# Graph attention in f32: keys on the partitions, heads packed into the array's row and column groups, the mask as a factor

## Chip, cores, metric

One core of a Trainium2 chip. The metric is device time in microseconds of one execution; medians of several executions are given. All runs told of here were in the fast state. Ratios are the mean time of one kernel's fast runs over that of the other's of the same rounds, so they are not quite the ratio of the medians quoted.

## The reference, cut to what matters

32 graphs of 512 nodes with 256 channels, f32 throughout. Two layers of masked attention with 8 heads of 32 channels; in layer 0 the mask is the symmetrised graph with its diagonal, in layer 1 the directed graph. Layer 0 has an MLP of 1,024 channels as well, and norms stand between.

```python
# layer 0 (inside: attention, norm, MLP, norm), then layer 1
x = _layernorm(x + _L0_gnn_ref(x, adj, ...))
x = _layernorm(x + _L1_gnn_ref(x, adj, ...))
# attention in both, with q, k, v as [graph, head, node, 32]
scores = einsum(q, k) / sqrt(32)
scores = where(allowed, scores, -inf)
out = einsum(softmax(scores), v)
```

## The kernel before

Two graphs are in work at a time, as two streams of pieces that a scheduler puts in order on each engine. Queries are on the partitions. For 128 queries and two heads:

```python
for j in range(2):                                   # L229: the mask, added in PSUM
    nc.tensor.matmul(s[:, j, :], ident_b, mask[:, i, :], start=True, stop=False)
for j, h in enumerate(heads):                        # L232: scores, 32 rows of the array
    at = slice((h % HPC) * HD, (h % HPC + 1) * HD)
    nc.tensor.matmul(s[:, j, :], qT[at, ...], kT[at, ...], start=False, stop=True)
nc.vector.tensor_reduce(top[...], s, AX.X, ALU.max, negate=True)            # L235
for j, h in enumerate(heads):                        # L238: exp, and the row sums
    nc.scalar.activation(p[:, j, :], s[:, j, :], AF.Exp, bias=top[:, h:h+1], accum_out=total[:, h:h+1])
# ... later, for each head
for k in range(NQ):                                  # L249: p transposed
    nc.tensor.transpose(ps[:, k*P:(k+1)*P], p[:, j, k*P:(k+1)*P], ident)
evict(pT, ps)                                        # L130 / L132, ScalarE and VectorE in turn
for k in range(NQ):                                  # L253: 32 columns for each 128-column weight
    nc.tensor.matmul(acc[:, h*HD:(h+1)*HD], pT[:, k*P:(k+1)*P], v[:, k, h*HD:(h+1)*HD], ...)
```

## Time and profile before

| | before |
|---|---|
| median | 10,242 us (10,190 to 10,266) |
| span in the profile | 10,250 us |
| TensorE busy | 10,080 us, 98% |
| VectorE / ScalarE / GpSimd busy | 3,223 / 2,375 / 1,234 us |
| mean granted TensorE clock | 0.711 |

A busy TensorE row is not an array at its peak: the same matmul takes twice as long at half the granted clock (one head's scores 1.051 us and 2.001 us, medians of this trace). So the clock is read beside the busy time. The prediction below quotes the lines.

### The profile page before, as it was taken

Reading aid. Unit: us, or ns where it says so; the run is one execution under the profiler, and the core shown is the slowest. Engines: PE = TensorE matmul, PEld = TensorE weight load, DVE = VectorE, ACT = ScalarE, POOL = GpSimd, SP = SyncE. Lnnn points to the kernel's source line nnn. Section 1 sums busy time; section 2 is a strip of 40 time slices with the busy share of each in tenths; the row PEclk is TensorE's granted clock in tenths of the full one; section 3 lists DMA queues with packets and bytes.
Section 4 is the critical chain, followed back from the end, with each engine's and each line's share of the span. In section 5 each row is a group of like instructions: output and inputs, shape, how many; then the busy total and the mean of one; then the engine's idle time right before and its main releaser. Section 6 shows DMA issues by size and latency. Waiting matters only on the chain.

```text
span 10250.1 us, 92945 instructions
## 1 busy us (share of the span) xinstructions
PE 10079.9 (98%) x38912; PEld 6353.5 (62%) x38912; DVE 3223.0 (31%) x5233; ACT 2374.8 (23%) x5681; POOL 1233.6 (12%) x1575
## 2 busy tenths in 40 slices
PE   9999999999999999999999999999999999999999
PEld 5666666656666666666666666666666666666665
DVE  2333333333332333323333233332333323333232
ACT  1222222222222222222222222222222222222221
POOL 2001111011110111101111011110011100111000
PEclk7667777677776777767777677776677767777666
DMA  1000000000000000000000000000000000000000
GB/s 44 7 3 9 9 9 7 3 9 9 9 7 3 9 9 9 7 3 9 9 9 9 1 9 9 9 9 5 5 9 9 9 5 5 9 9 5 1 3 5
DMA packets 57477, 78.44 MB, mean 8 GB/s; under 512 B 3936, under 2 KB 40160, under 8 KB 57056
## 3 DMA queue, kind: packets, MB, share of 16 engines
q1 hardware_dynamic: 57056, 72.50, 2.2%
q8 instruction: 304, 4.98, 0.2%
q14 instruction: 117, 0.96, 0.0%
HBM read 55.71 MB, written 16.78 MB: 7 GB/s over the span
## 4 chain that ended last, share of the span: by engine, by line
PE 92%; DVE 4%; POOL 3%; issue 1%; ACT 1%; DMA 0%; POOLq 0%; ACTq 0%; SPq 0%; DVEq 0%
PE psS L232 26%; PE psA L253 25%; PE psP L249 14%; PE psS L229 7%; PE psH L320 5%; PE psQK L197 4%; PE psO L279 4%; PE psF L330 2%; PE psV L206 2%; PE psC L274 1%; DVE top L235 1%; POOL rs L142 1%; PE psT L166 1%; POOL edge L176 1%; DVE st L139 1%; POOL rs L141 1%
## 5 line engine op out<-in xcount | busy, mean ns | idle before, releaser
L253 PEld LDWEIGHTS psA<-v,pT 128*128 128x128 f32 x16384 | 2723.0, 252 | 1250.5 <-issue 794.7
L232 PE MATMUL psS<-kT,qT 32*128 32x512 f32 x4096 | 2906.4, 911 | 0.0
L253 PE MATMUL psA<-v,pT 128*128 128x32 f32 x16384 | 2814.8, 329 | 69.4 <-DVE pT L132 60.9
L235 DVE TENSOR_REDUCE top<-psS 128x2 f32<-128x1024 f32 x1024 | 1253.0, 1224 | 2741.9 <-PE psS L232 2741.9
L249 PEld LDWEIGHTS psP<-ident,p 128*128 128x128 f32 x8192 | 1383.2, 198 | 696.0 <-issue 573.2
L238 ACT ACTIVATE p<-psS,top 128x512 f32<-128x512 f32 x2048 | 1392.5, 687 | 1549.0 <-DVE top L235 1544.3
L249 PE MATMUL psP<-ident,p 128*128 128x128 f32 x8192 | 1700.1, 363 | 36.2 <-ACT p L238 22.7
L130 ACT COPY pT<-psP 128x512 f32<-128x512 f32 x1024 | 599.0, 585 | 4191.8 <-PE psP L249 4191.0
L232 PEld LDWEIGHTS psS<-kT,qT 32*128 32x128 f32 x4096 | 719.6, 251 | 691.8 <-issue 663.5
L132 DVE COPY pT<-psP 128x512 f32<-128x512 f32 x1024 | 703.3, 687 | 1213.4 <-PE psP L249 1210.1
L229 PE MATMUL psS<-m,ident_b 128*128 128x512 bf16 x2048 | 983.8, 542 | 0.0
L141 POOL TENSOR_SCALAR rs<-mv 128x1 f32<-128x1 f32 x512 | 171.5, 335 | 5692.2 <-DVE mv L140 5692.2
L320 PE MATMUL psH<-xT,w_L_gnn_W 128*128 128x512 f32 x1024 | 503.0, 624 | 0.1
L279 PE MATMUL psO<-w_L_gnn_Wo,ctxT 128*128 128x256 f32 x1024 | 473.6, 611 | 15.0 <-ACT ctxT L130 8.3
L330 PE MATMUL psF<-w_L_gnn_W,hT 128*128 128x256 f32 x2048 | 475.5, 383 | 0.0
L279 PEld LDWEIGHTS psO<-w_L_gnn_Wo,ctxT 128*128 128x128 f32 x1024 | 281.4, 299 | 309.0 <-issue 104.4
L330 PEld LDWEIGHTS psF<-w_L_gnn_W,hT 128*128 128x128 f32 x2048 | 382.0, 190 | 79.4 <-issue 28.3
L265 DVE TENSOR_TENSOR ctx<-psA,rec 128x256 f32<-128x256 f32 x256 | 108.4, 423 | 1022.6 <-PE psA L253 1022.6
L238 ACT ACTIVATION_READ_ACCUMULATOR p<-psS,top 128x1 f32 x2048 | 412.4, 201 | 0.0
L352 POOL TENSOR_SCALAR nan<-top 128x1 f32<-128x1 f32 x128 | 30.1, 235 | 2907.3 <-DVE top L235 2906.0
L229 PEld LDWEIGHTS <-ident_b 128*128 128x128 bf16 x2048 | 294.0, 146 | 70.1 <-issue 27.5
L320 PEld LDWEIGHTS psH<-xT,w_L_gnn_W 128*128 128x128 f32 x1024 | 190.3, 199 | 178.3 <-issue 152.4
(63 smaller groups left out, 4537.0 us busy)
## 6 DMA issues: line engine op xcount, KB each, us to landing
adj<-in_adj_dram SPq DMA_DIRECT2D x32, 1024.0 KB, 5.2
x<-in_x_dram SPq DMA_DIRECT2D x32, 512.0 KB, 3.7
out_dram<-o SPq DMA_DIRECT2D x32, 512.0 KB, 2.9
w_L_gnn_W<-in_L_gnn_W_dram SPq DMA_DIRECT2D x2, 1024.0 KB, 10.5
w_L_gnn_Wqkv<-in_L_gnn_Wqkv_dram SPq DMA_DIRECT2D x1, 768.0 KB, 8.0
w_L_gnn_Wo<-in_L_gnn_Wo_dram SPq DMA_DIRECT2D x2, 256.0 KB, 7.3
s_L_gnn_bo<-in_L_gnn_bo_dram SPq DMA_DIRECT2D x2, 128.0 KB, 6.7
s_L_gnn_ln_g<-in_L_gnn_ln_g_dram SPq DMA_DIRECT2D x2, 128.0 KB, 6.0
```

Of the source, the lines that this page charges most:

```text
L130: nc.scalar.copy(dst, src)
L132: nc.vector.tensor_copy(dst, src)
L197: nc.tensor.matmul(ps[:, j, :], w[:, i, c * P : (c + 1) * P], xT[:, i, :], start=(i == 0), stop=(i == ND - 1))
L229: nc.tensor.matmul(s[:, j, :], ident_b, mask[:, i, :], start=True, stop=False)
L232: nc.tensor.matmul(s[:, j, :], qT[at, h // HPC, i * P : (i + 1) * P], kT[at, h // HPC, :], start=False, stop=True)
L235: nc.vector.tensor_reduce(top[:, 2 * hp : 2 * hp + 2], s, AX.X, ALU.max, negate=True)
L238: nc.scalar.activation(p[:, j, :], s[:, j, :], AF.Exp, bias=top[:, h : h + 1], accum_out=total[:, h : h + 1])
L249: nc.tensor.transpose(ps[:, k * P : (k + 1) * P], p[:, j, k * P : (k + 1) * P], ident)
L253: nc.tensor.matmul(acc[:, h * HD : (h + 1) * HD], pT[:, k * P : (k + 1) * P], v[:, k, h * HD : (h + 1) * HD], start=(k == 0), stop=(k == N ...
L279: nc.tensor.matmul(ps[:, :D], cT[:, k * P : (k + 1) * P], wo[layer][:, k, :], start=(k == 0), stop=(k == ND - 1))
L320: nc.tensor.matmul(ps, w1[:, c, f * P : (f + 1) * P], x1T[:, c, :], start=(c == 0), stop=(c == ND - 1))
L330: nc.tensor.matmul(ps[:, :D], hT[:, f, i * P : (i + 1) * P], w2[:, f, :], start=(f == 0), stop=(f == NF - 1))
```

## The change

It turns the scores around: keys on the partitions, queries along the free dimension. Then exp's output is already laid out as the moving operand of the product with v, and no transposes are needed. Four heads are taken together: their scores use the four groups of 32 rows of the array, their products with v the four groups of 32 columns. The mask becomes a factor on exp's output. The row sums, which now run across partitions, come from matmuls with ones. The row maximum is dropped; a check on the sums sends inputs for which that would fail to a general path behind a branch (not taken here). The core of the diff (cut: pools, layout of projections, norms two chunks at a time, the general path):

```diff
-            for j in range(2):
-                nc.tensor.matmul(s[:, j, :], ident_b, mask[:, i, :], start=True, stop=False)
-            for j, h in enumerate(heads):
-                nc.tensor.matmul(
-                    s[:, j, :], qT[at, h // HPC, i * P : (i + 1) * P], kT[at, h // HPC, :], start=False, stop=True
-                )
-            nc.vector.tensor_reduce(top[:, 2 * hp : 2 * hp + 2], s, AX.X, ALU.max, negate=True)
+                for j in range(HPC):
+                    at = slice(j * HD, (j + 1) * HD)
+                    nc.tensor.matmul(
+                        s[:, j, :], kT[at, hg, kc * P : (kc + 1) * P], qT[at, hg, :], start=True, stop=True
+                    )
+                nc.scalar.activation(p, s, AF.Exp, scale=SCALE)
+                nc.vector.tensor_tensor(p, p, mask[:, kc, None, :].to_broadcast([P, HPC, N]), ALU.mult)
...
-                for k in range(NQ):
-                    nc.tensor.transpose(ps[:, k * P : (k + 1) * P], p[:, j, k * P : (k + 1) * P], ident)
-                evict(pT, ps)
+                for j in range(HPC):
+                    h = hg * HPC + j
+                    nc.tensor.matmul(a[j * HD : (j + 1) * HD, :], v[:, kc, h * HD : (h + 1) * HD], p[:, j, :], ...)
+                for j in range(HPC):
+                    nc.tensor.matmul(s[j * HD : (j + 1) * HD, :], ones, p[:, j, :], ...)
...
-        for _ in range(24):
+        for _ in range(22):
             next(streams[0])
```

The score buffer is now single (four PSUM banks), and so are the two accumulators. In the profile of the changed kernel L252 is the scores, L256 exp, L257 the multiplication by the mask, L271 the products, L279 the row sums.

## The prediction

> **What bounds the kernel now.** I read the page first: part 1 (busy shares), part 2 (the slices), part 4 (the chain of waits), then the groups.
>
> ```profile
> PE 10079.9 (98%) x38912; PEld 6353.5 (62%) x38912; DVE 3223.0 (31%) x5233; ACT 2374.8 (23%) x5681; POOL 1233.6 (12%) x1575
> ...
> PEclk7667777677776777767777677776677767777666
> ...
> PE 92%; DVE 4%; POOL 3%; issue 1%; ACT 1%; DMA 0%; POOLq 0%; ACTq 0%; SPq 0%; DVEq 0%
> ```
>
> TensorE is busy 98% of the span and is 92% of the chain; nothing else is over 31%. DMA is nothing. But the granted clock is only six to seven tenths, so the tensor work is not only long, it runs slowed. The groups say which work it is:
>
> ```profile
> L253 PEld LDWEIGHTS psA<-v,pT 128*128 128x128 f32 x16384 | 2723.0, 252 | 1250.5 <-issue 794.7
> L232 PE MATMUL psS<-kT,qT 32*128 32x512 f32 x4096 | 2906.4, 911 | 0.0
> L253 PE MATMUL psA<-v,pT 128*128 128x32 f32 x16384 | 2814.8, 329 | 69.4 <-DVE pT L132 60.9
> L249 PE MATMUL psP<-ident,p 128*128 128x128 f32 x8192 | 1700.1, 363 | 36.2 <-ACT p L238 22.7
> L229 PE MATMUL psS<-m,ident_b 128*128 128x512 bf16 x2048 | 983.8, 542 | 0.0
> ```
>
> Scores 2.91 ms, products with v 2.81, transposes of the weights 1.70, mask matmuls 0.98: 8.4 of the 10.08 ms busy are attention. An f32 matmul has two records in these rows (2,048 score matmuls, 4,096 records). The product streams 32 columns per 128-column weight load, so it is a weight-load loop.
>
> Next, the timeline of TensorE at two places, one at full and one at half clock (start, length, what):
>
> ```profile
> 5005.99 1.13 PE L232 MATMUL psS<-kT,qT 32*128 32x512 f32 x4
> 5007.05 1.09 PE L249 MATMUL psP<-ident,p 128*128 128x128 f32 x8
> ...
> 5052.57 2.07 PE L232 MATMUL psS<-kT,qT 32*128 32x512 f32 x2
> 5054.58 0.47 PE L249 MATMUL psP<-ident,p 128*128 128x128 f32 x1
> ```
>
> At full clock two heads (4 records) in neighbouring row groups hold the array 1.06 us (5005.99 to 5007.05). At half clock one head (2 records) holds it 2.01 us. Over all such places in the trace the medians are 1.051 us for one head and 1.058 for two at full clock, 2.001 and 2.008 at half. So two row groups already run truly beside each other in f32, the second for 7 ns; but only some 300 of the 1,024 pairs stand together in the order, the others are split by other matmuls.
>
> Last, the table by stage, two stretches (columns: us, busy of each engine, PEclk, DMA share, GB/s):
>
> ```profile
> 5043.00:5091.00 48.00, 48.00 (x137) 29.00 (x136) 9.91 (x13) 9.56 (x25) 0.00 (x0) 0.51 0.00 0
> 5255.00:5320.00 65.00, 60.26 (x292) 39.80 (x290) 26.71 (x55) 15.31 (x30) 23.00 (x23) 1.00 0.09 25
> ```
>
> In the first there is only attention: TensorE is busy without a gap and still gets half the clock. In the second, MLP and projections run beside attention and it gets all of it. I sorted the 3.41 us steps of the granted clock by what streamed in them. Matmuls with 128x128 weights decide: a full-clock step is followed by full clock if they stream for over about a quarter of it, a half-clock step if they stream for over about 0.6 (97% of the steps fall so). K=32 scores alone and the 32-column products count almost nothing.
>
> **What the Trainium skill says.** "TensorE: Matmul & The Clock Gate", Part 3 (Packing small matmuls): four K=32 row tiles gave 3.07x, three M=32 column tiles 2.38x. The trace agrees for two row tiles in f32 (1.058 us for both); it has no column tile. Same page, Part 1 (The HAM clock gate): the clock follows how busy the array was in a 3.4 us window. The step length agrees, "busy" does not: 48.00 us of 48 busy ran at 0.51. "TensorEngine Tiling (Array Packing)", Key Properties: changing the tiling mode drains the array; scores followed by 128x128 work at a pitch of 1.06 us show no costly drain here, column mode is not shown. "VectorE: DVE Perf Modes", The perf-mode tier table: f32 tensor_tensor has no faster mode, 2,293 ns for 2,048 elements; the trace agrees at 1,024 (row of v from psV: 1,224 ns).
>
> **The change, part by part.** It removes per graph the mask matmuls, the transposes of p with their evictions (pT: 599 us ScalarE, 703 us VectorE in all), the maxima (1,253 us VectorE), the separate accumulator reads (412 us ScalarE) and psC. It adds, per 128 keys and four heads, one step: 4 score matmuls (K=32, four row groups), one exp over 128x2048, one multiply by the mask, 4 products (M=32, four column groups) and 4 row sums (ones as weights, same column groups). 32 graphs x 2 layers x 2 head groups x 4 key chunks = 512 steps.
>
> TensorE at full clock. A packed group of four: 1.051 + 3 x 0.007 = 1.07 us; assumed for the columns too. A step has three groups: 3.2 us, x512 = 1.64 ms. What stays, from the full-clock pitches in the trace: psH and psQK 1,024 matmuls of 512 columns x 0.88 us = 0.90 ms; psV and psO 1,024 of 256 columns x 0.43 = 0.44; psF 1,024 x 0.43 = 0.44; psT 0.09; psM 0.06, and psN, added, 512 x 0.056 = 0.03. Sum 1.96 ms. Floor: 3.60 ms.
>
> VectorE: multiply 512 x 2.29 = 1.17 ms; end of a head group 128 x (two transposes and a multiply of 512 at 0.69, reciprocal 0.2) = 0.29; norms as in their rows (217 + 91 + 248 + 105 us) and the sums before them (0.13), m0 0.09. About 2.3 ms. ScalarE: copies of 512 and 1,024 cost 585 and 1,016 ns, that is 0.84 ns an element and 154 fixed, so exp of 2,048 about 1.9 us, x512 = 0.97; hT 0.18; q and k 256 x 0.69 = 0.18; v, xT, m1 448 x 0.6 = 0.26. About 1.6 ms. GpSimd under 1 ms. All lie beside TensorE.
>
> The score buffer is single (4 banks), so scores, exp (1.07 + 1.9 + waits) repeat at no less than 3.2 us; with the multiply (2.3) and the products behind it, two steps take about 1.07 + 1.9 + 2.3 + 2.1 and waits = 7.8 us, 3.9 a step. One piece of the other graph's dense work (1.75 us for a pair of psH) stands between, 3.2 + 1.75 = 4.95 of TensorE, so the chain hides where the streams mix well. For split groups, the wait for the single accumulators at each head group's end, and evictions queued behind a 1.9 us exp, I add 15%: 4.1 ms if the clock stays full.
>
> **The rivals.** (a) **The clock halves in attention.** For it: K=32 and 32-column work counted nothing before. Against it: four groups together fill the array, and the dense half of each window keeps a full clock once there. If it comes, steps cost 3 x 2.02 = 6.1 us, 3.1 ms, and some 60% of the dense work beside them doubles, 3.1 ms: 6.3 ms. (b) **Column groups do not overlap in f32.** The trace has none. Then 8 x 0.9 + 1.07 = 8.3 us a step, 4.2 + 1.96 = 6.2 ms at full clock, up to 10 or more at half. (c) **The order splits the groups**, as it split 7 of 10 pairs before. Each group broken once adds 3.2 us a step, 1.6 ms: 5.5 ms. (d) **VectorE or the chain becomes the bound**: 2.3 ms and 512 x 3.9 = 2.0 ms are both under the floor, so only waits come of it.
>
> **Range and chances.** I give the packed, full-clock way 6 in 10 (about 4.1 to 4.6 ms, since some steps will be split or cold), (a) a quarter (5.2 to 6.3), (b) one in ten (6.2 to 10.5), and the rest to (c). The middle of that is 4,600 us; the tenth and ninetieth parts are at 3,900 and 6,600. Slower than now needs (b) with the clock halved: 0.03. Within 2% 0.01, faster 0.96.
>
> **What would show it.** Right: TensorE busy some 85 to 95% with PEclk at 0.8 or more; three pitches of about 1.07 us per step in the timeline; exp near 1.9 us, the multiply near 2.3; VectorE about half busy. Wrong: product records that follow each other at 0.4 us or more within a group (b); PEclk at five tenths under a busy TensorE (a); score groups in pieces of two or three matmuls (c); TensorE idle, waiting for the multiply or exp, in over a fifth of the span (d).

## The result

The median is 4,832 us (4,829 to 4,834): 0.471 of the time before, 95% interval 0.470 to 0.473. The output is correct.

The page of the changed kernel, the same three lines as quoted of the kernel before:

```profile
PE 3936.1 (82%) x20490; PEld 1763.5 (37%) x20490; DVE 2243.5 (46%) x3141; ACT 1564.9 (32%) x1473; POOL 1165.5 (24%) x1001
...
PEclk9999999999999999999999999999999999999998
...
PE 61%; DVE 22%; POOL 8%; ACT 7%; issue 2%; DMA 0%; SPq 0%; DVEq 0%; POOLq 0%; ACTq 0%
```

TensorE is busy 3,936 us instead of 10,080, the clock is near full in every slice (mean 0.925), and TensorE no longer is the whole chain: 22% of it is VectorE. The groups of attention (columns: line, engine, operation, output<-inputs, shape, count, busy us, mean ns, idle before, released by):

```profile
L257 DVE TENSOR_TENSOR p<-p,m 128x2048 f32<-128x2048 f32 x512 | 1173.6, 2297 | 1160.5 <-ACT p L256 1160.5
L256 ACT ACTIVATE p<-psS 128x2048 f32<-128x2048 f32 x512 | 961.2, 1877 | 996.0 <-PE psS L252 844.9
L271 PE MATMUL psA<-p,v 128*32 128x512 f32 x4096 | 599.6, 653 | 323.2 <-DVE p L257 255.8
L252 PE MATMUL psS<-qT,kT 32*128 32x512 f32 x4096 | 648.6, 670 | 117.9 <-ACT p L256 114.4
...
L279 PE MATMUL psR<-p,ones 128*32 128x512 f32 x4096 | 604.1, 623 | 30.5 <-DVE sT L286 26.5
```

The attention matmuls hold 1.85 ms together instead of 8.4; the records' mean of 623 to 670 ns against a busy time of some 150 ns a record says that four run at once. The multiply and exp are at 2,297 and 1,877 ns. The idle column has grown: TensorE waits 323 us before products and 118 before scores, against 69 and 0 in the kernel before. One step in the timeline, between dense work of the other graph:

```profile
2576.69 1.14 PE L252 MATMUL psS<-qT,kT 32*128 32x512 f32 x8
2577.76 1.07 PE L271 MATMUL psA<-p,v 128*32 128x512 f32 x8
2578.65 1.04 PE L279 MATMUL psR<-p,ones 128*32 128x512 f32 x8
2579.62 1.98 PE L227 MATMUL psQK<-xT,w_L_gnn_Wq 128*128 128x512 f32 x4
```

Eight records are four f32 matmuls. The scores start at 2576.69, the products at 2577.76, the sums at 2578.65, the next work at 2579.62: 1.07, 0.89 and 0.97 us. Over all such places at full clock the medians are 1.071, 0.882 and 0.972.

Where TensorE's time goes now: from each record's start and the clock granted then, some 3,462 us of its busy time are at full clock and 465 at half; 891 us of the span (4,827 less 3,936) it is idle. The kernel before has 4,201 us at full clock, 5,879 at half and 170 idle. Counted at full clock, as an estimate, the work fell from 7.14 to 3.69 ms, what half clock adds to it from 2.94 to 0.23, and idle time rose by 0.72: of the 5.4 ms gained, about half is the clock. The waits of TensorE by releaser show of what (us in total, times, longest):

```profile
PE psA L271 <- DVE p L257: 255.8, 137, 6.2
PE psT L186 <- DVE x L134: 151.4, 17, 9.6
PE psS L252 <- ACT p L256: 114.4, 62, 2.0
PE psT L186 <- DVE x L143: 98.4, 48, 2.5
PE psA L271 <- DVE cT L293: 65.0, 48, 1.8
```

The third line, and at 2717.70 the first, can be seen in the timeline where attention of both graphs falls together. There is nothing dense to put between:

```profile
2712.22 2.29 DVE L257 TENSOR_TENSOR p<-p,m 128x2048 f32<-128x2048 f32 x1 [1.89 <-ACT p L256]
...
2712.24 1.14 PE L252 MATMUL psS<-qT,kT 32*128 32x512 f32 x8
2713.44 1.88 ACT L256 ACTIVATE p<-psS 128x2048 f32<-128x2048 f32 x1 [1.26 <-PE psS L252]
2715.35 2.29 DVE L257 TENSOR_TENSOR p<-p,m 128x2048 f32<-128x2048 f32 x1 [0.84 <-ACT p L256]
...
2715.37 1.14 PE L252 MATMUL psS<-qT,kT 32*128 32x512 f32 x8 [2.00 <-ACT p L256]
...
2717.70 1.93 PE L271 MATMUL psA<-p,v 128*32 128x512 f32 x8 [1.19 <-DVE p L257]
```

TensorE is idle 2.00 us until exp has emptied the single score buffer: scores to scores in 3.13 us, with nothing in between.

The second line of the waits is another thing, 16 waits of some 9.5 us, once for each two graphs:

```profile
2665.21 5.37 POOL L193 TENSOR_SCALAR edge<-adj 128x2048 bf16<-128x2048 int32 x1 [3.88 <-PE psM L205]
...
2666.38 3.14 DVE L142 SCALAR_TENSOR_TENSOR cent<-yf,mv,s_L_gnn_ln_g 128x256 f32<-128x256 f32 x2
2670.55 0.22 POOL L127 TENSOR_SCALAR rs<-mv 128x2 f32<-128x2 f32 x1
...
2676.44 0.71 PEld L186 LDWEIGHTS psT<-ident,x 128*128 128x128 f32 x4 [9.81 <-DVE x L134]
```

A mask piece of 5.37 us stands ahead of the norm's 0.22 us operation in GpSimd's queue; the norms wait for that and TensorE for the norms. The two operations on VectorE took 3.14 us meanwhile (the first 2.74, the second 0.47), where one took 0.49 before. "SBUF — State Buffer", Who interferes with whom, of the Trainium skill, states that a VectorE operation with two SBUF inputs contends with a GpSimd operation that reads SBUF. This place agrees, but neither shuts the other out until its record ends: the first ended 1.45 us before the mask piece did, and the second was not slowed. No run took it apart; the stagger run below shows the multiply slowed in the same way.

### The profile page after: what moved, and what is told of

Read it like the earlier page. It is cut to its first block, busy times and chain, and to the rows that moved or that the text cites. A ratio compares the mean times of both kernels' runs of the same rounds, so it can differ in the third digit from the quotient of the medians.

```text
span 4827.4 us, 47999 instructions
## 1 busy us (share of the span) xinstructions
PE 3936.1 (82%) x20490; PEld 1763.5 (37%) x20490; DVE 2243.5 (46%) x3141; ACT 1564.9 (32%) x1473; POOL 1165.5 (24%) x1001
## 4 chain that ended last, share of the span: by engine, by line
PE 61%; DVE 22%; POOL 8%; ACT 7%; issue 2%; DMA 0%; SPq 0%; DVEq 0%; POOLq 0%; ACTq 0%
PE psA L271 10%; PE psH L341 10%; PE psQK L227 9%; DVE p L257 9%; PE psR L279 9%; PE psS L252 7%; PE psF L353 7%; ACT p L256 5%; PE psV L237 3%; POOL rs L128 3%; DVE st L125 3%; PE psO L313 2%; POOL edge L193 2%; PE psT L186 1%; POOL z L361 1%
## 5 line engine op out<-in xcount | busy, mean ns | idle before, releaser
L257 DVE TENSOR_TENSOR p<-p,m 128x2048 f32<-128x2048 f32 x512 | 1173.6, 2297 | 1160.5 <-ACT p L256 1160.5
L256 ACT ACTIVATE p<-psS 128x2048 f32<-128x2048 f32 x512 | 961.2, 1877 | 996.0 <-PE psS L252 844.9
L271 PE MATMUL psA<-p,v 128*32 128x512 f32 x4096 | 599.6, 653 | 323.2 <-DVE p L257 255.8
L252 PE MATMUL psS<-qT,kT 32*128 32x512 f32 x4096 | 648.6, 670 | 117.9 <-ACT p L256 114.4
L279 PE MATMUL psR<-p,ones 128*32 128x512 f32 x4096 | 604.1, 623 | 30.5 <-DVE sT L286 26.5
L186 PE MATMUL psT<-ident,x 128*128 128x128 f32 x768 | 170.9, 343 | 298.2 <-DVE x L134 151.4
L271 PEld LDWEIGHTS psA<-p,v 128*32 128x32 f32 x4096 | 90.9, 112 | 735.2 <-DVE p L257 491.2
L252 PEld LDWEIGHTS psS<-qT,kT 32*128 32x128 f32 x4096 | 175.5, 191 | 479.8 <-issue 266.2
L344 ACT ACTIVATE hT<-psH,c_L_gnn_b 128x512 f32<-128x512 f32 x256 | 175.9, 687 | 524.8 <-PE psH L341 524.8
L279 PEld LDWEIGHTS psR<-p,ones 128*32 128x32 f32 x4096 | 144.1, 116 | 419.3 <-issue 339.7
L313 PE MATMUL psO<-w_L_gnn_Wo,cT 128*128 128x256 f32 x1024 | 264.0, 391 | 14.6 <-ACT xT L187 10.8
L227 PE MATMUL psQK<-xT,w_L_gnn_Wqkv 128*128 128x512 f32 x512 | 241.6, 595 | 0.0
```

Source lines behind the costliest of these rows:

```text
L186: nc.tensor.transpose(ps[:, k * P : (k + 1) * P], src[:, k, c * P : (c + 1) * P], ident)
L227: nc.tensor.matmul(ps, w[:, i, c * P : (c + 1) * P], xT[:, i, :], start=(i == 0), stop=(i == ND - 1))
L252: nc.tensor.matmul(s[:, j, :], kT[at, hg, kc * P : (kc + 1) * P], qT[at, hg, :], start=True, stop=True)
L256: nc.scalar.activation(p, s, AF.Exp, scale=SCALE)
L257: nc.vector.tensor_tensor(p, p, mask[:, kc, None, :].to_broadcast([P, HPC, N]), ALU.mult)
L271: nc.tensor.matmul(a[j * HD : (j + 1) * HD, :], v[:, kc, h * HD : (h + 1) * HD], p[:, j, :], start=(kc == 0), stop=(kc == NQ - 1),)
```

## The experiments

My theory: the gain is TensorE work taken away and packed, at a clock that the packed work keeps up; what is left over the sum of TensorE's work is waits for exp, the multiply and the norms, where no dense work is beside. The rivals are named in each run.

### Packing undone: head by head

```diff
                 for j in range(HPC):
                     nc.tensor.matmul(s[:, j, :], kT[...], qT[...], start=True, stop=True)
+                    if before is not None:
+                        multiply(*before, j)      # product and row sum of head j, one step behind
```

> The changed kernel with its TensorE order broken: for each head score, product, row sum, then the next head, so that no two neighbours can share the array as groups of four do (some pairs of a row sum and the next head's score or product still may). Same instructions and result. If packing is what makes the change fast (my theory): a step costs about 12 x 0.85 to 1.05 us instead of 2.93, so 512 x 7 to 9 us more, 8.3 to 9.8 ms at full clock, and the clock falls too, since single K=32 scores and single 32-column products count little. Rival, that the gain is from the removed transposes, masks and maxima alone and packing hardly matters: under 5.5 ms.

Measured: 6,417 us, ratio 0.626, clock 0.929. Neither side had it. The order shows why: the scheduler often issued scores or products together all the same, when one kind was ready before the other. So I counted places, that is sets of attention records of one kind (scores, products or sums), each starting within 60 ns of the one before: 3,254 in the changed kernel, 6,430 here (some 20 more with a limit of 40 ns). TensorE's busy time grew by 1,613 us for 3,176 places, 0.51 each. Where a head did stand alone, nothing overlapped:

```profile
2600.46 1.04 PE L272 MATMUL psA<-p,v 128*32 128x512 f32 x2
2601.34 1.02 PE L279 MATMUL psR<-p,ones 128*32 128x512 f32 x2
2602.30 1.12 PE L252 MATMUL psS<-qT,kT 32*128 32x512 f32 x2
2603.35 1.04 PE L272 MATMUL psA<-p,v 128*32 128x512 f32 x2
```

Two records are one matmul here. One head takes 2.89 us (from product to product, 2600.46 to 2603.35), as much as four heads packed (2.93 us). The clock stayed up, to which I come below.

### Column groups in turn

```diff
-                for j in range(HPC): product of head j
-                for j in range(HPC): row sum of head j
+                for j in range(HPC): product of head j, row sum of head j
```

> The changed kernel with products and row sums in turn, head by head (product 0, sum 0, product 1, sum 1, ...), score groups of four kept. Unlike in the run before of this kind, the order of the program keeps this turn throughout. A product and its sum use the same column group and cannot overlap; a sum and the next head's product can. Theory (column groups overlap whenever neighbours differ in group): five places of about 0.9 us instead of two, 512 x 2.7 us = 1.4 ms more TensorE work, 5.9 to 6.4 ms. Second reading (once a group is followed by itself nothing overlaps): eight places, 512 x 5.4 = 2.8 ms more, 7.2 to 7.9 ms. Rival (packing of columns is worth little): under 5.2 ms. Clock: the broken order showed single column matmuls of 128 rows keep it up, so 0.92 or more.

Measured: 4,864 us, ratio 0.475 (the changed kernel: 0.471). All three readings of "what overlaps" fell, and the rival's number came out without its reason. The timeline shows that packing was not lost at all (eight records a group again):

```profile
2564.92 1.09 PE L271 MATMUL psA<-p,v 128*32 128x512 f32 x8
2565.80 1.06 PE L278 MATMUL psR<-p,ones 128*32 128x512 f32 x8
```

The program has product 0, sum 0, product 1, sum 1, after the scheduler too (1,815 of 2,048 products are followed at once by the sum of the same head); in the trace all four products start within 41 ns of each other (2564.92 to 2564.96), and all four sums 0.43 us after the products' second pass. It looks as if each column group worked off its own list beside the others. Product 1 started before sum 0, which is ahead of it in the program. So what undid packing in the run before was not the turn but the change between scores and products, row groups and column groups.

### Packing undone, products two steps behind

Products two steps behind have their input ready, so the broken order is kept more often; the stagger of 13 is explained below. The kernel to compare with is the same with packing left (next but one, 4,576 us).

```diff
+                    old = ahead.pop(0) if len(ahead) == 2 else None
-                    p = scores(hg, kc, ahead)
+                    p = scores(hg, kc, old)
```

> The head-by-head order (score, product, row sum) again, with the products two steps behind and the stagger of 13, so that most of the order stays broken; beside the same kernel unbroken, 4,576 us. In the first broken order every step to and from a score cost a place of its own (score 1.05, product and sum 1.83 us a head), but half of the heads had stayed together: 3,193 more places of 0.48 us for 1.58 ms. Theory (time follows the number of places): each further place costs 0.48 us; with three quarters of the heads apart some 6,500 to 7,500 places more than unbroken, 7.7 to 8.3 ms. Rival (other waits absorb it): under 6.8 ms. Clock: if rows of 128 in use keep the clock, whatever the columns, it stays over 0.9; if filling the array does, it falls under 0.75.

Measured: 6,913 us, ratio 0.674, clock 0.962, TensorE busy 95%. The number of places was again smaller than I had guessed, 8,670 against 3,734 in the packed one: 4,936 more. The price of a place was right: 2,337 us more time, 0.47 us a place. So the time follows the number of places, and the 6.8 ms of the rival is passed. Without any overlap there would be 12,288 places, 9,034 more than in the changed kernel; at 0.47 us that would be 4.2 ms more, an estimate that no run reached. By it the change without its packing would take about 9.1 ms, so most of the 5.4 ms gained hangs on packing. The clock does not: with packing undone it was 0.962.

### The stagger of the two streams

A graph has 57 pieces, and the streams take turns by piece.

```diff
-        for _ in range(22):
+        for _ in range(13):
```

> The changed kernel with the second stream of graphs started 13 pieces after the first instead of 22. A graph has 57 pieces, attention is pieces 14 to 22 and 47 to 55; 22 apart, one attention of each graph falls on one of the other's, and then nothing dense fills the waits for exp and the mask; 13 apart, none does. Theory (the 0.87 ms of TensorE's idle time comes of attention beside attention and dense beside dense): idle falls by a third to two thirds, 4.25 to 4.6 ms, clock over 0.95. Rival (the waits are inside each graph's own chain, whatever runs beside): within 2% of 4,832 us.

Measured: 4,685 us, ratio 0.457, clock 0.923: 3% faster, less than expected; idle time fell from 891 to 731 us, under a fifth. TensorE's wait for exp fell from 114 us to 21, so attention beside attention is what that wait is. But the waits for the multiply rose (products 256 to 335, sums 4 to 74 us). The trace shows why: the multiply now runs beside GpSimd's mask pieces.

```profile
360.67 5.37 POOL L193 TENSOR_SCALAR edge<-adj 128x2048 bf16<-128x2048 int32 x1 [19.27 <-PE psM L205]
360.75 5.71 DVE L257 TENSOR_TENSOR p<-p,m 128x2048 f32<-128x2048 f32 x1
...
366.61 1.08 PE L279 MATMUL psR<-p,ones 128*32 128x512 f32 x4 [4.90 <-DVE p L257]
```

Of the 512 multiplies 60 are stretched in this way, each ending about 0.42 us after a mask piece, and 141 of the 409 us that TensorE waits for the multiply stand directly behind one. In the changed kernel no multiply ran beside a mask piece. So the new stagger removed one collision and made another; without it the wait is as large as before (268 us against 260), and there the rival holds.

### Products two steps behind the scores

```diff
-                    if ahead is not None:
-                        product(*ahead)
-                    ahead = (hg, kc, p)
+                    if len(ahead) == 2:
+                        product(*ahead.pop(0))
+                    ahead.append((hg, kc, p))
```

(with the stagger of 13)

> The stagger of 13 with the products two steps behind the scores instead of one. With the stagger of 13 TensorE still waited 409 us for the multiply. Theory (that wait is one of slack: the multiply queues behind the other graph's norms on VectorE): it falls to under 100 us, and the half-clock time with it, 4.25 to 4.5 ms. Rival (the program's order is set so that the wait moves to exp and the score buffer): within 2% of the stagger alone, 4,685 us.

Measured: 4,576 us, ratio 0.446, clock 0.945; 2.3% under the stagger alone, a little over the range. Waits for the multiply fell from 409 to 103 us, and the next wait took part of the gain, that of the sums for the single accumulator to be emptied:

```profile
PE psR L279 <- DVE sT L286: 140.6, 32, 6.8
PE psA L271 <- DVE p L257: 103.0, 50, 3.9
```

The norms that the theory names were not the main thing: 60 multiplies are stretched beside mask pieces here too, and 58 us of the wait stand behind them. The further step gives slack for whatever holds the multiply up.

This is the fastest version that keeps f32 throughout, 5% under the changed kernel.

### The multiply taken away, and done twice

```diff
-                nc.vector.tensor_tensor(p, p, mask[:, kc, None, :].to_broadcast([P, HPC, N]), ALU.mult)
```

> The changed kernel without the multiplication by the mask (wrong result on purpose). VectorE loses 1.17 ms and each step's chain 2.3 us. Theory (the multiply is off the path except where attention stands beside attention): the 256 us for which products waited for it and part of the half-clock time go, 4.4 to 4.65 ms. Rival (the chain of exp and multiply sets the pace): it falls by a good part of 1.17 ms, below 4.2 ms. Third: nothing, within 2%.

Measured: 4,518 us, ratio 0.441, clock 0.939, and a wrong result as intended. 314 us of the multiply's 1,174 us busy time come back: within the expected range, neither the whole nor nothing.

```diff
+                nc.vector.tensor_tensor(p, p, mask[:, kc, None, :].to_broadcast([P, HPC, N]), ALU.mult)
```

> The changed kernel with the multiplication by the mask done twice (0 or 1, so the result stays right): VectorE gains 1.17 ms, to some 3.4 ms, each step's chain 2.3 us. Without the multiply the time fell by 314 us. Theory (the multiply matters only where nothing dense stands beside attention or where it queues behind the norms): 300 to 800 us more, 5.1 to 5.6 ms. Rival (the chain sets the pace now): 1.0 ms or more, over 5.8 ms.

Measured: 5,722 us, ratio 0.558, clock 0.862. 890 us more, between theory and rival. A second multiply is dearer than the first is worth: the step's chain passes the room that the dense work beside it gives. TensorE's waits for it went from 256 us to this:

```profile
PE psA L272 <- DVE p L258: 723.5, 300, 6.0
```

The clock adds to it: TensorE's busy time at half clock rose from 465 to 1,094 us, since idle steps let the clock fall and the work after them is slow.

### One part alone: the kernel before without its maximum

```diff
-            nc.vector.tensor_reduce(top[:, 2 * hp : 2 * hp + 2], s, AX.X, ALU.max, negate=True)
...
-                    p[:, j, :], s[:, j, :], AF.Exp, bias=top[:, h : h + 1], accum_out=total[:, h : h + 1]
+                    p[:, j, :], s[:, j, :], AF.Exp, accum_out=total[:, h : h + 1]
```

(also a memset of the tile that held the maxima, since a later check reads it)

> The kernel before with its row maximum alone taken out (exp without a bias, as in the changed kernel; right for these inputs). Theory (TensorE at a halved clock bounds the kernel before, the maximum lies beside it): within 2% of 10,242 us, although VectorE loses 1.25 ms. Rival (the maximum delays exp and so the transposes): 3 to 10% faster.

Measured: 10,825 us, ratio 1.060, clock 0.681. Slower, which neither side had. The maximum is off the path, as said: VectorE is busy 2,033 us instead of 3,223 and nothing is gained. But with it gone the scheduler made another order, and the order bears on overlap and clock.

```profile
PE 10524.7 (97%) x38400; PEld 6707.3 (62%) x38912; DVE 2033.0 (19%) x4465; ACT 2189.9 (20%) x5681; POOL 1246.5 (12%) x1575
...
PEclk7567676777767677676776667767567665766666
```

Score records in overlapping pairs (of 4,096) fell from 1,204 to 708, and TensorE's busy time at half clock rose from 5,879 to 6,713 us. That fits the direction; that the order is the cause is not shown, since I did not run a kernel that changes the order alone.

### Two bytes for exp's output

```diff
-                p = work.tile([P, HPC, N], F32, tag="p", ...)
+                p = work.tile([P, HPC, N], BF16, tag="p", ...)
```

(also v and the ones in bfloat16; stagger of 13)

> The stagger of 13 with exp's output, v and the ones in bfloat16: the multiply has two-byte operands only, and products and row sums pass the array once. The relative error will be larger, perhaps too large. Theory: the multiply falls to about 1.2 us from 2.3, product and sum groups to about 0.25 us each from 0.88 and 0.97, 512 x 1.35 = 0.69 ms less TensorE work: 3.7 to 4.1 ms, TensorE busy under 3.4 ms. Rival (exp and the single score buffer then set the pace): no faster than 4.3 ms, TensorE idle over a quarter.

Measured: 4,139 us, ratio 0.404, correct by the same comparison; clock 0.889. Just over the range. TensorE's busy time, 3,421 us, is near what was expected; the multiply was not always 1.2 us (60 of the 512 were stretched beside mask pieces; duration in ns: least, median, most):

```profile
L259 DVE TENSOR_TENSOR p<-p,m x512: 1181/1225/4368, 57.4 to 4117.0; 128x2048 bf16<-128x2048 bf16 x171
```

With the products two steps behind as well, and a fourth buffer for exp's output:

> bfloat16 weights, stagger of 13 and products two steps behind, together. Theory (the 253 us wait for the multiply and the half-clock time after it are slack): 3.75 to 4.0 ms. Rival (the norms' chain, VectorE to GpSimd, bounds by then): within 2% of 4,139 us.

Measured: 4,032 us, ratio 0.393, clock 0.892. 2.6% under the one before it, short of 4.0 ms. It is the fastest of all, but it rounds the attention weights and v to bfloat16, which the kernels before and after do not.

## Why the prediction was right, point by point

**What bounds the kernel before**: right. Taking 1.2 ms off VectorE gained nothing.

**A packed group of four**: right in kind, better in size. Scores 1.071 us against 1.07 said; the column groups, assumed at the same, took 0.882 and 0.972. A step is 2.93 us instead of 3.2. The undone packings show that this is no side effect: each place lost cost 0.47 us of time or more. The sign given for it, three pitches of about 1.07 us, held for one of the three.

**The other engines**: exp 1.88 us (1.9 said), the multiply 2.30 (2.29), VectorE 2.24 ms (2.3), ScalarE 1.56 (1.6). GpSimd took 1.17 ms instead of under 1: some of its operations got longer, perhaps beside a busier VectorE, which no run took apart (the 128x1024 addition of the MLP's bias took 2,347 ns at the median before and 3,348 after).

**Rival (a), the clock**: it did not come, and the prediction's rule for it was too narrow. It said that K=32 scores and "the 32-column products" count almost nothing. The latter was an effect of the kernel before, whose products stream 32 columns past 128x128 weights. The broken orders show it (steps of 3.41 us of the granted clock, sorted by what streamed: a pass of 512 f32 columns counts 0.427 us at full clock, the pitch of the trace). In 209 full-clock steps of the first broken kernel and 695 of the second hardly anything but single matmuls streamed, scores with 32 rows, products and sums with 128 rows and 32 columns, and all but one, which streamed for only 0.38 of the step, were followed by full clock. In the first, 32 such steps were at half clock: in all 17 that were followed by full clock single products and sums streamed for 0.83 of the step or more, in the other 15 for 0.51 or less, with single scores for 0.39 or more beside. So full rows lift the clock, whatever the columns; single scores of 32 rows beside them did not.

Four score groups together do count. In the changed kernel, full-clock steps with other work for 0.12 to 0.25 of the step kept the clock in 56 of 56 cases with packed scores for 0.25 or more beside, and in 0 of 19 with scores for under 0.1. One rule fits the full-clock steps of all kernels: weigh the streaming time by the share of the 128 rows in use, one score a quarter and four together 1; a full-clock step keeps the clock when this is over 0.38 of the step. In each of the twelve traces 98% or more of the full-clock steps fall so, those of the kernel before too, where streaming time alone sorts 89% at best. That is a sorting of traces; no run changed the rows alone.

**Rival (b), columns not overlapping**: wrong, as given the small chance. **Rival (c), split groups**: small here; 3,254 places against 3,072 if none were split. **Rival (d), chain and VectorE as waits**: came as waits, in size the miss of the prediction: TensorE was busy 82% of the span, under the 85 to 95% given as a sign of being right, and idle for 18%.

**The term that was too small.** The sum was 3.60 ms of TensorE work plus 15%, 4.1 ms, and 4.6 as the middle over the ways. The measured 4.83 ms lies above the 4.1 to 4.6 that this way was given. Measured: 3.46 ms busy at full clock, plus half of the 465 us at half clock, is 3.69 ms of work, 0.09 over. The allowance for waits was 0.5 ms; it measured 0.89 ms of idle time, and the clock that falls in idle steps added the other half of the 465, 0.23 ms. That is 1.1 ms for 0.5. I had reasoned that a dense piece stands beside a step where the streams mix well (4.95 us of TensorE against 3.9 of chain). At a stagger of 22 pieces the two graphs' attentions fall together for a part, and there the single score buffer sets the pace. That is the smaller part: the new stagger won 147 us, with its new collision in it. The waits for the multiply (256 us) and for the norms (250 us, the second and fourth lines of the waits), which the sum had not priced singly, are the larger. The middle was near the result only because chances for worse ways were mixed in.

## What to carry to other kernels

Count TensorE's work in places where groups of heads run at once, and read from the order that groups stay together: going between row groups and column groups is what ends the overlap, not the turn of products and sums. When TensorE stops being the whole chain, its idle time costs twice, by the wait and by the clock after it (0.89 and 0.23 ms here); so give two streams a stagger in which one's chain meets the other's dense work, and put one more step between a producer on another engine and the matmul that needs it. After such a move look for new collisions on other engines, as that of the multiply with the mask pieces.

## What the Trainium skill lacked or had wrong

- "TensorE: Matmul & The Clock Gate", Part 1: the clock is told as following how busy TensorE is, without saying what counts as busy. The kernel before had 48.00 us of 48 busy in the profile at 0.51. By the sorted steps, rows in use decide (over 0.38 of a step keeps full clock): single matmuls of 128 rows and 32 columns kept or lifted the clock, single ones of 32 rows did not lift it.
- Same page, Part 3: matmuls are said to start and end strictly in the order of the program. With products and sums in turn, product 1 started before sum 0; each column group ran as if by its own list, and the time was 4,864 us against 4,832.
- Same page, Part 3: 3.07x for four row tiles, 2.38x for three column tiles. Here, f32 and 512 columns, four scores took 1.071 us against 1.051 for one, and four products 0.882 against 0.882 for one: by these pitches nearly fourfold. No run repeats the page's own case.
- "TensorEngine Tiling (Array Packing)", Key Properties: a change of mode is said to drain the array, without a figure. In the broken order the pitch from one matmul's second pass to the next matmul was 0.43 us from product to sum (same mode) and 0.52 from sum to score and from score to product.
- "SBUF — State Buffer", Who interferes with whom: the page has no figure for this pair of operations. An f32 multiply over 128x2048 took up to 5.72 us beside a GpSimd mask piece instead of 2.29.
- No page tells that taking work off an engine that is not the bottleneck can cost time: 6% here, with the maximum gone, probably through the order of the scheduler.
